# Four-layer transformer block: attention probabilities moved by pairs of units, the last groups' mask and part of their transposes on TensorE, closing steps spread over more units

## Chip, cores and metric

The kernel runs on one core of one Trainium2 chip. The metric is the device time of one execution in microseconds (us); three runs of the kernel before gave a median of 2282.05 us (2280.4 to 2284.7).

## What is computed

The input is x of 1024 tokens by 256 features, float32. Eight sublayers follow each other, each of the form x = layernorm(x + sublayer(x)): four attentions (called attn0 to attn3 here) and four feed-forward layers (ffn0 to ffn3). The change concerns attn1, attn3 and the start of the feed-forward layers. Both attentions have 16 heads of 128 features; attn3 has 4 key/value heads, each shared by 4 query heads, and normalises queries and keys per head.

```python
# attn1 (attn3 alike, with x @ Wq.T, per-head normalisation, k and v repeated, no biases)
logits = jnp.einsum('bhtd,bhds->bhts', q, k) * scale
mask = jnp.triu(jnp.full((t, t), -jnp.inf, dtype=x.dtype), k=1)
weights = jax.nn.softmax(logits + mask, axis=-1)
out = jnp.einsum('bhts,bhsd->bhtd', weights, v)
out = out.transpose(0, 2, 1, 3).reshape(b, t, h * dh)
return out @ Wo + bo
# ffn3: 64 experts, the 8 most probable of each token, and one shared expert
probs = jax.nn.softmax((h @ router_w.T).astype(jnp.float32), axis=-1)
top_vals, top_idx = lax.top_k(probs, TOP_K)
top_vals = top_vals / jnp.sum(top_vals, axis=-1, keepdims=True)
```

The one sequence has 1024 tokens, so a head has 8 blocks of 128 queries, and block b sees b + 1 blocks of keys.

## The kernel before

**Units.** In attn1 and attn3 the work is cut into 128 units each. A unit is one head and one block of 128 queries, with 1 to 8 blocks of keys. attn1 goes through 4 groups g of 4 heads, within a head through the two halves and the 4 blocks of each half. attn3 goes through 4 groups g (one key/value head each), within a group through the 8 blocks b, within a block through the 4 query heads h. Two consecutive units form a pair: in attn1 two neighbouring blocks of a head (n and n + 1 key blocks), in attn3 two heads of one block (equal sizes).

**One unit** (`Pipe.unit`) is a chain over all engines. `scores` (L307) multiplies queries and keys on TensorE into a PSUM tile of two banks, called wide; there are two of them. `exp_scores` adds the causal mask to the last 128 columns on VectorE (L243), takes the row maximum on VectorE (L248), in attn3 multiplies it by a factor on GpSimd (L250), and takes the exponential on ScalarE with the row sum beside it (L253). `norm_probs` takes the reciprocal of the sum on VectorE (L260) and multiplies on GpSimd (L261). `turn_probs` transposes 32x32 squares on VectorE into a tile called turned (L276), and four DMAs on SP's queue (L284) carry it into a tile pt, where it stands fully transposed. In attn1 each unit has its own turned tile and four DMAs (argument `both` false); in attn3 a pair shares one turned tile and four DMAs (`both` true). turned has two buffers. The product with the values (`values`, L298) runs per pair and is copied out by ScalarE (L1131 in attn1, L2050 in attn3).

**Order.** Inside both attentions the order of TensorE, ScalarE, VectorE, GpSimd and SP is the program's own order (`in_order`, transfers included), so an instruction that waits holds up all that follows it on its engine. `unit` emits, for unit u: reciprocal and division of unit u-1, scores of u, mask, maximum and exponential of u, then the transpose of u-1. Then `fill` hands TensorE as much other work as an allowance says (`left`, a base per unit plus a slope per key block): products with values of earlier pairs, output projections (`add_up`, L1107 in attn1; `project_heads`, L758 in attn3), projections of later keys, values and queries. `then` queues a pair's product with the values and frees it five units later (`Pipe.LAG`); a finished group of heads puts its `add_up` on the list `soon`, from which the next unit takes it. When nothing is left to hand out, TensorE has only the scores and the queued products.

**Closing.** In attn3's last group each finished pair of blocks starts a `close`, a generator of which one step runs per unit (`close_on`), one closing after the other: layer norm (L208), transposes of x (`transpose_two`, L173), the router's product (L161), softmax and top 8 on VectorE (L1879 to L1905), and for each of two halves of the experts a split into three bfloat16 parts on VectorE (`split3`, L387 to L389) and, in the same step, their transposes on TensorE (`transpose_comb`, L377). Steps left over when attn3 ends run at the start of ffn3, through the argument `before` of `ffn`.

**Feed-forward.** `ffn` runs chunks of hidden units over the first half of the tokens and, `Kit.LAG` = 2 chunks later, over the second half. Here a scheduler sets the order on each engine; the kernel gives only the program's sequence. ffn1 has a loop of its own with the same LAG.

The helper lines L154, L161 (projections), L173 (transposes) and L307 serve several stages.

Of the kernel before, what the change touches and what calls it, by code (L numbers as in the profile page):

```python
# [24 lines left out]
BF16 = mybir.dt.bfloat16  # L25
# [6 lines left out]
P = 128  # L32
# [4 lines left out]
HALF = 512  # L37
# [5 lines left out]
class Kit:  # L43
# [62 lines left out]
    def constants(self):  # L106
# [8 lines left out]
        make_causal_mask(nc, self.causal, mask_val=NEG)  # L115
        self.ones = const("ones", [P, 1])
# [122 lines left out]
    def exp_scores(self, scores, n, scale=None):  # L239
# [3 lines left out]
        nc.vector.tensor_tensor(  # L243
            scores[:, n - P : n], scores[:, n - P : n], self.causal, ALU.add
        )
# [17 lines left out]
    def turn_probs(self, probs, blocks, pt, slot, both):  # L263

        nc = self.nc
        n = blocks * P  # L270
        if not both or slot == 0:
            self.turned = self.tile("turned", [P, (1 + both) * 2 * HALF])
        squares = self.turned[:, : (1 + both) * n].rearrange(
            "p (b s k q) -> p s b k q", b=4, s=1 + both, q=32
        )
        nc.vector.transpose(  # L276
            squares[:, slot if both else 0],
            probs[:, :n].rearrange("p (k i b) -> p b k i", b=4, i=32),
        )
        if both and slot == 0:  # L280
            return
        slots = slice(0, 2) if both else slice(slot, slot + 1)
        for a in range(4):
            nc.sync.dma_start(  # L284
                out=pt.rearrange("p (s a) r -> p a s r", a=4)[:, a, slots, : n // 4],
                in_=self.turned[a * 32 : a * 32 + 32, : (1 + both) * n].rearrange(
                    "i (b s r) -> i b s r", b=4, s=1 + both
                ),
            )

    def probs_tile(self, blocks):

        n = min(n for n in self.pt_bufs if n >= blocks)
        return self.tile("pt", [P, 8, n * 32], tag=f"pt{n}", bufs=self.pt_bufs[n])

    def values(self, out, value, pt, b, last, first=0):

        self.nc.tensor.matmul(  # L298
            out[:, first * P :].rearrange("p (s q) -> p s q", q=32), lhsT=value,
            rhs=pt[:, first * 4 :, b * 32 : b * 32 + 32], start=b == 0, stop=last,  # L300
        )

    def scores(self, query, key, n):
        s = self.wide()
        for lo in range(0, n, HALF):
            m = min(HALF, n - lo)
            self.nc.tensor.matmul(  # L307
                s[:, lo : lo + m], lhsT=query, rhs=key(lo, m), start=True, stop=True
            )
        return s  # L310
# [3 lines left out]
    LAG = 2  # L314

    def ffn(self, chunks, count, hidden, before=iter(())):
# [8 lines left out]
        def add_up(i, half):  # L325
            size, gate, up, down, more = held[i] if half == 0 else held.pop(i)
            g, u = self.bank()[:size], self.bank()[:size]
            self.project(g, gate, half * HALF, HALF)
            self.project(u, up, half * HALF, HALF)
            h = hidden(g, u, half, more)  # L330
# [6 lines left out]
        for i in range(count + self.LAG):  # L337
# [3 lines left out]
            for _ in before:  # L341
                pass
# [60 lines left out]

COLUMN = 1 / 600


class Pipe:
# [8 lines left out]
    def __init__(self, k, base, slope, more, both=False):  # L416
        self.k, self.base, self.slope, self.more, self.both = k, base, slope, more, both
        self.pairs = 0
        self.soon = []
        self.first, self.rest, self.queued, self.left = None, [], [], 0.0  # L420
# [5 lines left out]
    def unit(self, query, key, blocks, pt, slot, scale=None):  # L426
        k = self.k
        before = self.norm()
        sc = k.scores(query, key, blocks * P)
        probs, inv = k.exp_scores(sc, blocks * P, scale)  # L430
        self.first = (probs, blocks * P, inv, pt, slot)
# [3 lines left out]
    def norm(self):  # L435
        before, self.first = self.first, None
# [5 lines left out]
    def turn(self, before):  # L442
# [5 lines left out]
        for q in self.queued:  # L448
            q[0] -= 1
# [1798 lines left out]
```

## Time and profile before

| what | value |
|---|---|
| median of three runs | 2282.05 us (2280.4 to 2284.7) |
| the profiled execution's own time | 2276.97 us |
| its span, first to last instruction | 2275.3 us |
| TensorE busy (matmul records) | 2065.0 us, 91% |
| VectorE / ScalarE / GpSimd busy | 1325.2 / 856.9 / 528.2 us |
| mean granted TensorE clock | 0.965 of full |
| moved by DMA | 166.74 MB in 200804 packets |

Stages by their own lines: attn0 to about 294 us, ffn0 to about 408, attn1 to about 920, ffn1 to about 985, attn2 to 1214, ffn2 to about 1398, attn3 to about 1895, ffn3 to the end. A float32 matmul appears in the records as two passes, so a 128x512 product is two records. "Idle before" in a row is the time the engine stood before those instructions, and the name after the arrow is what ended it. A busy TensorE isn't a TensorE at full pace: passes are pipelined and a granted clock of 0.5 doubles them.

### The profile page before, as it was taken

How to read it: one execution, taken by the hardware profiler on the slowest of the kernel's cores; microseconds unless marked ns; L12 is line 12 of the kernel's file. 1: busy time of each engine (PE TensorE's matmuls, PEld its weight loads, DVE VectorE, ACT ScalarE, POOL GpSimd, SP SyncE). 2: the span in 40 equal slices, each digit the busy share in tenths (PEclk: the TensorE clock that was granted, in tenths of full speed). 3: DMA queues.
4: the chain of work that ended last, by engine and by line, in shares of the span. 5: the costliest groups of instructions: out<-in, count | busy, mean ns of one | idle time of the engine just before them, and what ended most of it. 6: DMA issues, size and time to landing. Idle time of an engine off the chain costs nothing.

```text
span 2275.3 us, 25208 instructions
## 1 busy us (share of the span) xinstructions
PE 2065.0 (91%) x7955; PEld 1211.8 (53%) x7955; DVE 1325.2 (58%) x2687; ACT 856.9 (38%) x2230; POOL 528.2 (23%) x805
## 2 busy tenths in 40 slices
PE   8999769799999997988888999899998778999997
PEld 4666545466676665754434444466666444444443
DVE  5677646567776777456744444476767774222223
ACT  3666624443343433444452224544443321111111
POOL 4333221333333333402110001333333220000000
PEclk9999879899999999979999999999999989999999
DMA  4100054254545544105000010244445441111100
GB/s 160 36 10 29 29 169 121 65 136 110 139 112 151 151 111 117 38 28 177 2 2 10 28 29 1 48 90 111 96 103 112 104 95 39 37 40 44 30 2 19
DMA packets 200804, 166.74 MB, mean 73 GB/s; under 512 B 71680, under 2 KB 176192, under 8 KB 200672
## 3 DMA queue, kind: packets, MB, share of 16 engines
q1 hardware_dynamic: 191088, 140.07, 24.0%
q0 software_dynamic: 9584, 25.05, 3.7%
q8 instruction: 65, 1.06, 0.2%
q14 instruction: 67, 0.55, 0.1%
HBM read 68.72 MB, written 17.17 MB: 38 GB/s over the span
## 4 chain that ended last, share of the span: by engine, by line
PE 67%; DVE 15%; ACT 6%; DMA 4%; issue 4%; POOL 2%; SPq 1%; DVEq 0%; ACTq 0%; POOLq 0%
PE bank L154 23%; PE wide L307 8%; PE wide L332 8%; PE bank L298 7%; PE bank L161 4%; DVE turned L276 3%; ACT e L692 3%; PE bank L758 2%; DMA pt<-turned 2%; PE bank L1107 2%; PE bank L1544 1%; PE bank L938 1%; PE bank L1282 1%; DVE st L684 1%; PE bank L747 1%
## 5 line engine op out<-in xcount | busy, mean ns | idle before, releaser
L154 PE MATMUL bank<-xT,w 128*128 128x512 f32 (+2 forms) x1520 | 659.8, 567 | 4.1 <-DVE xT L180 2.6
L154 PEld LDWEIGHTS bank<-xT,w 128*128 128x128 f32 (+1 forms) x1520 | 287.9, 194 | 272.6 <-issue 250.7
L276 DVE STREAM_TRANSPOSE turned<-p 128x128 f32<-128x128 f32 (+7 forms) x256 | 312.8, 1222 | 122.1 <-DMA pt<-turned 87.0
L307 PE MATMUL wide<-k,q 128*128 128x512 f32 (+3 forms) x768 | 294.1, 493 | 29.6 <-ACT p L253 28.7
L261 POOL TENSOR_SCALAR p<-p,st 128x128 f32<-128x128 f32 (+7 forms) x256 | 190.4, 744 | 503.0 <-DVE st L260 502.5
L298 PE MATMUL bank<-pt,v 128*128 128x256 f32 x1216 | 282.0, 375 | 7.5 <-DMA pt<-turned 5.0
L298 PEld LDWEIGHTS bank<-pt,v 128*128 128x128 f32 x1216 | 231.5, 194 | 61.9 <-issue 20.0
L307 PEld LDWEIGHTS wide<-k,q 128*128 128x128 f32 x768 | 141.2, 191 | 152.2 <-issue 93.6
L248 DVE TENSOR_REDUCE st<-wide 128x1 f32<-128x128 f32 (+7 forms) x256 | 194.1, 758 | 8.8
L253 ACT ACTIVATE p<-wide,st,factor 128x128 f32<-128x128 f32 (+7 forms) x128 | 106.4, 831 | 235.0 <-POOL st L250 223.7
L2138 DVE TENSOR_TENSOR t<-t,bank 128x512 f32<-128x512 f32 (+1 forms) x66 | 45.4, 688 | 251.6 <-PE bank L154 251.0
L332 PE MATMUL wide<-t,w 128*128 128x512 f32 (+1 forms) x392 | 187.3, 600 | 4.5 <-DVE t L2139 2.8
L253 ACT ACTIVATE p<-wide,st 128x128 f32<-128x128 f32 (+7 forms) x128 | 94.9, 741 | 249.5 <-DVE st L248 229.4
L2137 ACT ACTIVATE t<-bank 128x512 f32<-128x512 f32 (+1 forms) x66 | 39.4, 597 | 306.2 <-PE bank L154 306.2
L161 PE MATMUL bank<-w,xT 128*128 128x512 f32 (+3 forms) x320 | 124.6, 525 | 2.9 <-DVE xT L180 2.9
L243 DVE TENSOR_TENSOR wide<-wide,causal 128x128 f32<-128x128 f32 x256 | 74.2, 290 | 89.7 <-PE wide L307 88.5
L332 PEld LDWEIGHTS wide<-t,w 128*128 128x128 f32 (+1 forms) x392 | 68.2, 189 | 108.6 <-issue 48.1
L692 ACT ACTIVATE e<-wide,st 128x128 f32<-128x128 f32 x256 | 90.1, 377 | 50.9 <-DVE st L684 34.4
L1569 ACT ACTIVATE pt<-wide 128x1024 f32<-128x1024 f32 (+3 forms) x96 | 75.7, 811 | 72.2 <-PE wide L1563 69.9
L161 PEld LDWEIGHTS bank<-w,xT 128*128 128x128 f32 x320 | 59.2, 208 | 48.5 <-issue 42.7
L2131 POOL COPY t<-select 99x128 bf16<-99x128 bf16 (+1 forms) x33 | 9.4, 292 | 319.8 <-PE bank L988 319.8
L235 DVE TENSOR_TENSOR x<-bank,x 128x256 f32<-128x256 f32 x120 | 48.1, 412 | 50.6 <-PE bank L747 21.1
(310 smaller groups left out, 2864.0 us busy)
## 6 DMA issues: line engine op xcount, KB each, us to landing
pt<-turned SPq DMA_DIRECT2D x96, 128.0 KB, 2.8
pt<-turned SPq DMA_DIRECT2D x96, 96.0 KB, 2.4
pt<-turned SPq DMA_DIRECT2D x32, 256.0 KB, 4.9
w<-in_L_ffn_gate_up_dram SPq DMA_DIRECT2D x16, 512.0 KB, 3.7
pt<-turned SPq DMA_DIRECT2D x64, 112.0 KB, 2.5
pt<-turned SPq DMA_DIRECT2D x32, 224.0 KB, 4.4
w<-in_L_attn_Wq_dram SPq DMA_DIRECT2D x12, 512.0 KB, 4.3
w<-in_L_attn_Wo_dram SPq DMA_DIRECT2D x12, 512.0 KB, 3.8
```

The costliest lines, as they stand in the source:

```text
L154: self.nc.tensor.matmul(out, lhsT=weight(c), rhs=self.xcols(c, lo, n), start=c == 0, stop=c == NC - 1)
L161: self.nc.tensor.matmul(out, lhsT=self.xcols(c, lo, n), rhs=weight(c), start=c == 0, stop=c == NC - 1)
L243: nc.vector.tensor_tensor(scores[:, n - P : n], scores[:, n - P : n], self.causal, ALU.add)
L248: nc.vector.tensor_reduce(top, scores[:, :n], axis=AX.X, op=ALU.max, negate=True)
L253: nc.scalar.activation(probs[:, :n], scores[:, :n], AF.Exp, bias=top, scale=1.0 if scale is None else scale, accum_out=total,)
L261: self.nc.gpsimd.tensor_scalar(probs[:, :n], probs[:, :n], total, 1.0, ALU.mult, ALU.mult)
L276: nc.vector.transpose(squares[:, slot if both else 0], probs[:, :n].rearrange("p (k i b) -> p b k i", b=4, i=32),)
L298: self.nc.tensor.matmul(out[:, first * P :].rearrange("p (s q) -> p s q", q=32), lhsT=value, rhs=pt[:, first * 4 :, b * 32 : b * 32 + 32], ...
L307: self.nc.tensor.matmul(s[:, lo : lo + m], lhsT=query, rhs=key(lo, m), start=True, stop=True)
L332: nc.tensor.matmul(acc[m][:, half * HALF : (half + 1) * HALF], lhsT=down[:, m * P : (m + 1) * P], rhs=h, start=i == 0, stop=i == count - 1,)
L692: nc.scalar.activation(e[:, r, f, b, :], sc[:, r, f, b, :], AF.Exp, bias=top[:, at : at + 1], accum_out=total[:, at : at + 1],)
L1569: nc.scalar.activation(two[:, :, lo:], sc[:, :, lo:], AF.Exp)
```

## The change

1. **Pairs.** A class `Pair` replaces `turn_probs`, `probs_tile` and `values`. Both attentions now write the two units of a pair side by side into one turned tile and send four DMAs per pair; in pt the two units lie side by side for each of the four rows of squares, so a DMA's runs are contiguous over the pair. In attn1 that makes 4 DMAs per pair where there were 8. turned is a little larger (15 x 128 and 16 x 128 columns, two buffers), pt a little smaller; attn1 keeps 11 value tiles in place of 12, one tile of the feed-forward weights' decoding is halved, and the order of value projections is shifted by one.
2. **Mask on TensorE.** For g = 3 in both attentions `scores` adds the mask by a bfloat16 product of an identity and the mask into the last 128 columns, and VectorE's addition is left out.
3. **Part of the transposes on TensorE.** For the pairs of head 3 of group 3 in attn1 (4 pairs) and of heads 2 and 3 of group 3 in attn3 (8 pairs) the probabilities are transposed by TensorE, up to four blocks per PSUM bank, and copied into pt by ScalarE; these pairs have neither VectorE transpose nor DMA. The steps run within `fill`, after its first piece of other work.
4. **Closing steps spread.** `close` has one more empty step after the norm, computes both splits in two steps, and only then issues the two transposes, a step each. In `ffn` the left-over steps are taken one after each projection of the first chunks, the rest after the third chunk; before, all were emitted after the first.
5. **Sums over heads two units later.** `soon` holds `[2, add_up]`: a group's output projection is freed two units after its last product, not one.
6. `Kit.LAG` is 3 in place of 2 (ffn1, ffn2, ffn3); a scratch tile of attn3 has one buffer in place of two.

```diff
-    def exp_scores(self, scores, n, scale=None):
+    def exp_scores(self, scores, n, scale=None, masked=False):
-        nc.vector.tensor_tensor(
-            scores[:, n - P : n], scores[:, n - P : n], self.causal, ALU.add
-        )
+        if not masked:
+            nc.vector.tensor_tensor(
+                scores[:, n - P : n], scores[:, n - P : n], self.causal, ALU.add
+            )
...
+        if masked:
+            self.nc.tensor.matmul(
+                s[:, n - P : n], lhsT=self.short_ident, rhs=self.short_causal, start=False,
+                stop=True, skip_group_check=True,
+            )
...
-    LAG = 2
+    LAG = 3
...
             self.project(g, gate, half * HALF, HALF)
+            next(before, None)
             self.project(u, up, half * HALF, HALF)
+            next(before, None)
...
-            for _ in before:
-                pass
+            if i == self.LAG - 1:
+                for _ in before:
+                    pass
...
+class Pair:
...
+    def turn(self, probs, slot):
+        k, n = self.k, self.blocks[slot] * P
+        if slot == 0:
+            self.turned = k.tile("turned", [P, k.turned])[:, : 4 * self.width]
+        squares = self.turned.rearrange("p (b r) -> p b r", b=4)[:, :, self.columns(slot)]
+        k.nc.vector.transpose(
+            squares.rearrange("p b (k q) -> p b k q", q=32),
+            probs[:, :n].rearrange("p (k i b) -> p b k i", b=4, i=32),
+        )
+        if slot == 1:
+            for a in range(4):
+                k.nc.sync.dma_start(
+                    out=self.pt[:, a, : self.width],
+                    in_=self.turned[a * 32 : a * 32 + 32, :].rearrange("i (b r) -> i b r", b=4),
+                )
+    def turn_on_pe(self, probs, slot):
+        k, blocks = self.k, self.blocks[slot]
+        to = self.pt[:, :, self.columns(slot)].rearrange("p a (k q) -> p k a q", q=32)
+        for lo in range(0, blocks, 4):
+            m = min(4, blocks - lo)
+            ps = k.bank()[:, : m * P]
+            for i in range(m):
+                k.nc.tensor.transpose(
+                    ps[:, i * P : (i + 1) * P], probs[:, (lo + i) * P : (lo + i + 1) * P], k.ident
+                )
+            k.nc.scalar.copy(
+                to[:, lo : lo + m], ps.rearrange("p (k a q) -> p k a q", a=4, q=32)
+            )
+            yield m * 0.13
...
     def fill(self):
         while self.left > 0:
             measure = self.step() or self.more()
+            while self.turning:
+                self.left -= self.turn_on()
...
-    k.pt_bufs = {4: 2, 8: 2}
+    k.pt_bufs, k.turned = {7: 2, 15: 2}, 15 * P
...
-            pipe.soon.append(add_up(g, half))
+            pipe.soon.append([2, add_up(g, half)])
...
+                pair = Pair(k, (blocks, blocks + 1), on_pe=(g, h) == (3, 3))
...
             k.norm_tile(t + i, stats[t // 4], rstd[:, i : i + 1])
         yield
+        yield
         k.transpose_two(t)
...
+        parts = [k.tile("t2", [P, 2, 3, 33]) for _ in range(2)]
         for group in range(2):
             yield
-            parts = k.tile("t2", [P, 2, 3, 33])
-            k.split3([parts[:, :, i, :] for i in range(3)], comb[:, :, group, :], [P, 2, 33])
-            k.transpose_comb(parts, k.combT[group], t)
+            k.split3(
+                [parts[group][:, :, i, :] for i in range(3)], comb[:, :, group, :], [P, 2, 33]
+            )
+        for group in range(2):
+            yield
+            k.transpose_comb(parts[group], k.combT[group], t)
...
-            pipe.soon.append(add_up(g, b, oT))
+            pipe.soon.append([2, add_up(g, b, oT)])
...
+                        pair = Pair(k, (b + 1, b + 1), on_pe=(g, h) == (3, 2))
...
-    attn1: dict(q=2, k=5, v=12, pt=2, p4=2, turned=2, ot=7, bv=1, prep=1),
+    attn1: dict(q=2, k=5, v=11, pt=2, p4=2, turned=2, ot=7, bv=1, prep=1),
```

## The prediction

> **What bounds the kernel now.** I read the page first, then the busy time by stage, then TensorE's waits, then the timeline of the worst place. The windows are attn1, attn3 to its last third, the end of attn3, and ffn3; columns are length, busy time and records of PE, PEld, DVE, ACT, POOL, then granted clock, DMA share, GB/s.
>
> ```profile
> 466.00:920.00 454.00, 435.50 (x1664) 301.81 (x1662) 327.59 (x635) 181.60 (x410) 156.62 (x211) 1.00 0.50 126
> ...
> 1440.00:1800.00 360.00, 332.45 (x1246) 217.70 (x1246) 260.27 (x502) 157.35 (x360) 128.51 (x232) 0.99 0.44 95
> 1800.00:1898.00 98.00, 66.97 (x240) 47.62 (x241) 65.42 (x162) 21.36 (x42) 19.43 (x38) 0.86 0.43 106
> 1898.00:2275.00 377.00, 361.03 (x884) 154.72 (x882) 107.88 (x201) 46.84 (x76) 8.43 (x29) 0.99 0.09 28
> ```
>
> TensorE is the bound nearly everywhere. Only the end of attn3 stands out: 31 of 98 us idle, and a clock of 0.86. So added TensorE work costs its full time in most places, and a gain must come from TensorE's idle time. TensorE's own waits name it:
>
> ```profile
> PE wide L307 <- ACT p L253: 28.7, 26, 6.5
> PE bank L377 <- DVE t L389: 28.7, 6, 8.3
> ...
> PE bank L758 <- ACT ot L2050: 8.0, 8, 1.7
> ...
> PE bank L298 <- DMA pt<-turned: 5.0, 4, 1.8
> ```
>
> The second row is the closing: six times TensorE stands in front of a 0.4 us transpose until VectorE has split its data. The first is scores waiting for the softmax chain to free a wide tile. Transfers cost TensorE 5.0 us in the whole kernel, although VectorE waits 87.0 us for them. How a closing stops everything:
>
> ```profile
> 1806.91 0.22 DVE L389 TENSOR_TENSOR t<-t,short 128x66 f32<-128x66 f32 x1
> 1807.19 0.41 PEld L377 LDWEIGHTS bank<-ident,t 128*99 128x99 f32 x2 [7.69 <-DVE t L389]
> 1807.19 0.75 PE L377 MATMUL bank<-ident,t 128*99 128x128 f32 x2 [7.29 <-DVE t L389]
> 1807.52 2.87 PEld L298 LDWEIGHTS bank<-pt,v 128*128 128x128 f32 x8
> 1807.73 3.06 PE L298 MATMUL bank<-pt,v 128*128 128x256 f32 x8
> ```
>
> After 7.29 us of standing, eight value passes take 3.06 us; at 1889.43 the same eight took 1.89. The gap is paid twice.
>
> **The skill.** "TensorE: Matmul & The Clock Gate", Part 1, says the array falls to half clock after an idle window of about 3.4 us and needs about 3.4 us of sustained work to return. The trace agrees: its clock records fall to 0.5 for 6.8 us after the gap of 7.29, for 10.2 us after that of 8.30, in all for 27.3 us in 1780 to 1900. The same page, Part 4, gives about 275 ns for a TensorE transpose in a kernel and says it doesn't count as work for the clock; here the same float32 transposes (L729) have durations of 282 ns but start 109 ns apart in runs of four, and I use 109. "DMA: Bandwidth & Descriptors", Specifications, asks for at least 512 B a transfer; 71680 of the 200804 packets are smaller, and pairs double the runs, but no TensorE time hangs on it. "ScalarE: Activation LUTs" puts a table load at 1283 ns; the trace has 1.28 us.
>
> **Pace.** From the distance of successive starts at full clock: a pass of 512 columns 429 ns, 256 columns 216, 128 columns 109, a bfloat16 product of 128 columns 66 (L1517, the mask product of attn2). A float32 product is two passes. For the two kinds that the change adds the upper bound is busy time by count: L729 20.2 us / 128 = 158 ns, L1517 18.6 / 128 = 145; over 108 transposes and 64 masks that would be 10.3 us more, and I keep it for the range. The lower bound is nothing, where they fall into idle time. "PE work" below is counts times these; "lost" is elapsed less PE work. The profiled execution took 2276.97 us, 5.1 less than the median of 2282.05; I take the saving from both alike.
>
> **A. Last group of attn3** (first row maximum at 1749.8, end of its last projection at 1894.9: 145.1 us). PE work before: scores 4 heads x 36 blocks x 2 x 109 = 30.9 (with rounding); values 31.1 and 9.8 of group 2's last pairs; ten projections of 1.72, 17.2; three closings of 1.8, 5.3: together 94.4. Lost 50.7: five waits of L377 (7.29+3.88+8.30+4.60+1.19 = 25.3), three of L173 on the norm (5.3), one on the copy of xT (2.1), others on ScalarE and one transfer 6.5, and half the 27.3 us at half clock, at most 13.7.
> Added: 32 masks x 66 ns = 2.1; 72 blocks (2 heads x 36) x 109 ns = 7.8. One closing fewer in this stretch (see B), -1.7. PE work after: 102.6.
> Removed from VectorE: 32 masks x 290 ns (row L243) = 9.3; transposes of 16 units, 2 x (0.41+0.63+0.87+1.11+1.33+1.59+1.81+2.03) = 19.6. VectorE is busy 74.4 of the 96.6 us from 1749.8 to 1846.4.
> The chain: VectorE takes a unit's mask only after the reciprocal of the unit before, which waits for its exponential, so a unit lasts mask, maximum, factor, exponential, reciprocal. At six blocks: masks at 1824.61 and 1827.96, 3.35 us, of which 0.6 is a closing's norm. Without mask and norm about 2.5, under TensorE's need in the new order of 2.9 to 3.0 for that size (11.6 for four units). So TensorE becomes the bound, and the closing's splits are made a unit or more ahead of their transposes. What is late next is the division on GpSimd: TensorE's transposes of unit u-1 stand after the scores of u and at most one piece, and wait for exponential, reciprocal (0.15) and division (0.91 at six blocks); behind them wait the next scores. The 16 units' ScalarE copies, some 24 of at most 0.61 us (row L731), stand behind the exponential on ScalarE and hold one or two of four PSUM banks. I allow 14 us lost: a third of the old waits of 14 (L173, xT, others) stays, 5; new waits 16 x 0.35, 5.5; clock 3.5. Bounds 8 (a tenth of the PE work) and 26 (half of the old loss). After: 102.6 + 14 = 116.6. **Saved 28.5** (16.5 to 34.5).
>
> **B. Start of ffn3.** A closing now has 10 to 11 steps, at one per unit, and 8 units per closing come in; so they pile up. The order of the built program confirms it: two closings, not one, stand after the last projection. The first of these lies between the chunks' projections, with some 8 us of them between its router product and its transposes: hidden. The second has its router product followed at once by its transposes on TensorE. Before, that distance was 5.2 us (1901.15 to 1906.36), with 1.94 us of products inside and 3.45 idle. Now about 5.2 idle and 0.7 for a product delayed behind VectorE's route steps, instead of 3.45 and 0.88; half clock follows either way. Loss 1.6, rounded to 2.0, and the closing's own 1.7 moved here. Two more table loads, 2 x 1.28, end under the projections. **Costs 3.7** (0 to 9).
>
> **C. Last group of attn1.** Up to unit 112 (849.5) TensorE never stands (window 800 to 850: no loss), so 16 masks cost 1.1. From 849.5 to 919.3 (69.8 us) PE work is 55.3, lost 14.5, by scores waiting on the chain. Added 16 masks 1.1 and 36 blocks x 109 ns = 3.9: 60.3. VectorE loses 0.29 a unit, and 9.8 of transposes in the last eight units. Lost after 6 (2 to 12): 66.3. Saved 3.5, less 1.1: **2.4** (-3.5 to 6.5).
>
> **D. Sums two units later.** The 8.0 us of L758 on ScalarE's copy: 5.2 lie in groups 0 to 2; three fifths return, **3.0** (0 to 5), since some turn into the wait for the chain.
>
> **E. Pairs.** In attn1 groups 0 to 2 TensorE loses 1.3 and 2.4 us of 108 (556 to 664, 664 to 772). VectorE's shorter waits gain nothing there. Transfers are later: a pair's values come four units after its transpose, some 14 us at 3.6 a unit, while transpose (2.0) and landing (4.9 for 256 KB, row of DMA issues) need 7. SP has 240 issues in attn1 for 512; its other issues move up. **0** (-3 to 3).
>
> **F. LAG 3**: the same chunks in the same steady order; ffn3 from 1920 to 2230 already loses only 0.2 us. **0** (-2 to 2).
>
> Sum: 28.5 - 3.7 + 2.4 + 3.0 = 30.2. Profiled 2246.8; median **2251.9**.
>
> **Rivals.** (1) New waits take half: transposes on TensorE wait 0.8 us in each of 24 units, 19 in place of 5.5 and 3: saving 20, time 2262 to 2270. For it: chain and TensorE are within a fifth of each other. Against: the PE-bound units let the division finish. (2) Slower: each of these 24 transposes is reached before its unit's exponential has started to be read, and TensorE stands through exponential, reciprocal and division, about 2.4 us at six blocks: 24 x 2.4 = 58, in place of 8.5, time about 2301. It decides against the change from 1.6 us per unit (30.2 / 24 on top of 0.35). Against: scores of u, mask and a piece of 1.7 us lie between. (3) The pile at ffn3's start exposes both closings, about 12 us more with clock: 2264. (4) VectorE's 87 us for transfers did hold attn1 back: its other 8.7 us lost (466 to 800) and most of the 6 in C go too: 2239. That the mask isn't moved is excluded by the instruction order.
>
> **Chances.** Forecast, 2238 to 2264: 0.68. Rival 1: 0.15. Rival 2: 0.04. Rival 3: 0.06. Rival 4: 0.07. Range 2238 to 2269: 2 in 10 left out. A measurement can tell 0.2% (4.6 us) from no change. Faster: 0.67 + 0.13 + 0.05 + 0.07 = 0.92; same 0.04; slower 0.04 (rival 2).
>
> **What would show it.** A right: waits of the comb transposes on the splits under 8 us in all, clock over 0.95 in attn3's last group, its stretch near 117 us, new waits of transposes on GpSimd near 0.35 us. B: one gap of about 5 us at ffn3's start. C: scores' waits on the exponential in attn1's end under 6. D: projections waiting on ScalarE's copy under 3 us. Wrong if the wait on the exponential grows past 28.7, or the division holds TensorE for over 1.6 us a unit.

## The result and the profile after

The changed kernel takes 2273.26 us (median of seven runs, 2268.97 to 2276.67). The kernel before, on the same chip beside it, takes 2280.40 us (seven runs, 2277.2 to 2285.86). The ratio is 0.9966, with a 95% interval of 0.9952 to 0.998: faster by some 7 us, where 30 were forecast. The profiled executions say the same, 2268.97 us against 2276.97, so they can be taken apart. Cut at the first row maximum of each group and at the last output projection of an attention:

| stretch | before, us | after, us | difference | forecast |
|---|---|---|---|---|
| start to attn1 | 440.7 | 442.7 | +2.0 | 0 |
| attn1, groups 0 to 2 | 348.2 | 351.5 | +3.3 | 0 (E) |
| attn1, last group | 130.5 | 139.5 | +9.0 | -2.4 (C) |
| ffn1, attn2, ffn2 | 509.4 | 509.6 | +0.2 | 0 (F) |
| attn3, groups 0 to 2 | 321.1 | 321.9 | +0.8 | -3.0 (D) |
| attn3, last group | 145.3 | 116.8 | -28.5 | -28.5 (A) |
| ffn3 | 380.2 | 385.2 | +5.0 | +3.7 (B) |

The last group of attn3 came out as forecast. Attn1 gave 12.3 us of it away, where a small gain was forecast. The first row is no effect of the change: over the kernels below, whose code is the same there, it lay between 439.5 and 444.0 us. The fourth varies as much, 505.8 to 515.0 us over the kernels with `Kit.LAG` 3 in every layer, at granted clocks of 0.98 to 0.95, and the lag's own 3 us (below) are lost in it. Attn1's four groups together took 490.8 to 494.0 us in four kernels that leave attn1 as changed, and 476.5 to 479.6 in five that have it as before (the kernel before among them), so a difference of one or two us between two executions is no finding.

The busy times by stage of the changed kernel, in the columns of the prediction's first fence: the last group of attn1, the last group of attn3, ffn3.

```profile
794.20:933.70 139.50, 127.05 (x528) 90.91 (x527) 77.00 (x147) 46.66 (x108) 46.23 (x66) 0.95 0.35 85
1765.10:1881.90 116.80, 105.78 (x492) 79.15 (x492) 70.84 (x180) 46.76 (x112) 33.80 (x74) 0.99 0.32 83
1881.90:2267.10 385.20, 367.59 (x906) 158.90 (x904) 115.41 (x238) 50.88 (x81) 9.28 (x32) 0.98 0.09 28
```

Attn3's end now runs at 0.99 of the clock and stands 11 of 117 us. It is attn1's last group that has the low clock, 0.95, and stands 12.5 us.

TensorE's waits in the changed kernel, longest in total first (engine and line, what it waited for: us in all, times, longest):

```profile
PE wide L274 <- ACT p L259: 17.5, 18, 6.5
PE bank L421 <- POOL p L267: 14.8, 7, 6.1
...
PE bank L439 <- DMA pt<-turned: 12.0, 11, 2.1
...
PE bank L353 <- DVE t L365: 5.2, 1, 5.2
PE wide L307 <- DVE t L1878: 4.8, 2, 2.4
...
PE bank L2041 <- ACT t L2033: 3.8, 4, 1.2
```

Row by row against before: scores that wait for the exponential fell from 28.7 to 17.5 us; the closing's transposes (L377 then, L353 now) from 28.7 in six waits to one of 5.2; output projections that waited for ScalarE's copy (L758, 8.0) are gone from the list. Four rows are new or grown: TensorE's own transposes wait 14.8 us for GpSimd's division, values wait 12.0 us for transfers instead of 5.0, ffn2's products 4.8 instead of 1.6 (L307, L332 before), and attn3's sums of squares 3.8 for ScalarE (L2041). Much of what the closings and the scores gave back, other waits took.

### The profile page after: what moved, and what is told of

It reads as the page before. It is cut to its first block, busy times and chain, and to the rows that moved or that the text cites. A ratio compares the mean times of both kernels' runs of the same rounds, so it can differ in the third digit from the quotient of the medians.

```text
span 2267.1 us, 24836 instructions
## 1 busy us (share of the span) xinstructions
PE 2073.2 (91%) x8127; PEld 1221.8 (54%) x8127; DVE 1284.3 (57%) x2599; ACT 872.9 (39%) x2268; POOL 528.9 (23%) x807
## 2 busy tenths in 40 slices
DMA packets 124255, 159.60 MB, mean 70 GB/s; under 512 B 28928, under 2 KB 96064, under 8 KB 124128
## 3 DMA queue, kind: packets, MB, share of 16 engines
q8 instruction: 65, 1.06, 0.2%
## 4 chain that ended last, share of the span: by engine, by line
PE 70%; DVE 13%; ACT 6%; DMA 4%; issue 3%; POOL 2%; SPq 2%; DVEq 0%; ACTq 0%; POOLq 0%
PE bank L159 23%; PE wide L274 8%; PE bank L439 8%; PE wide L307 8%; PE bank L166 4%; ACT e L749 3%; DMA pt<-turned 3%; DVE turned L402 2%; PE bank L1164 2%; PE bank L815 2%; PE bank L1601 1%; DVE st L741 1%; PE bank L995 1%; PE bank L1339 1%; POOL p L267 1%
## 5 line engine op out<-in xcount | busy, mean ns | idle before, releaser
L402 DVE STREAM_TRANSPOSE turned<-p 128x128 f32<-128x128 f32 (+7 forms) x232 | 283.6, 1223 | 84.2 <-DMA pt<-turned 48.2
L274 PE MATMUL wide<-k,q 128*128 128x512 f32 (+3 forms) x768 | 294.3, 493 | 18.4 <-ACT p L259 17.5
L307 PE MATMUL wide<-t,w 128*128 128x512 f32 x392 | 187.6, 601 | 8.2 <-DVE t L1878 4.8
L2201 DVE TENSOR_TENSOR t<-t,bank 128x512 f32<-128x512 f32 x66 | 45.3, 687 | 247.2 <-PE bank L159 247.2
L2200 ACT ACTIVATE t<-bank 128x512 f32<-128x512 f32 x66 | 39.4, 597 | 294.1 <-PE bank L159 279.7
L307 PEld LDWEIGHTS wide<-t,w 128*128 128x128 f32 x392 | 68.2, 189 | 113.4 <-issue 48.3
L249 DVE TENSOR_TENSOR wide<-wide,causal 128x128 f32<-128x128 f32 x192 | 55.9, 291 | 97.7 <-PE wide L274 96.4
```

Of the source, the lines that this page charges most:

```text
L249: nc.vector.tensor_tensor(scores[:, n - P : n], scores[:, n - P : n], self.causal, ALU.add)
L274: self.nc.tensor.matmul(s[:, lo : lo + m], lhsT=query, rhs=key(lo, m), start=True, stop=not masked or lo + m < n, skip_group_check=masked,)
L307: nc.tensor.matmul(acc[m][:, half * HALF : (half + 1) * HALF], lhsT=down[:, m * P : (m + 1) * P], rhs=h, start=i == 0, stop=i == count - 1,)
L402: k.nc.vector.transpose(squares.rearrange("p b (k q) -> p b k q", q=32), probs[:, :n].rearrange("p (k i b) -> p b k i", b=4, i=32),)
```

## The experiments

After the result two accounts were open. The theory: attn3's gain is the spread closing alone, and attn1 loses by two things, transposes on TensorE that wait for the division (C) and transfers by pairs that arrive later (E). The rivals: attn3 owes its gain to mask and transposes on TensorE; and attn1 loses by the added TensorE work, or by the eleven value tiles and the shifted order, rather than by waits. All twelve kernels are edits of the changed kernel; each ratio is to the kernel before, run on the same chip, so whole kernels are compared by their ratios. The code cuts show the lines that name an edit; what else it needs (the argument `alone` and its branch, shown once, buffer sizes, the lines of an edit described above) is left out at the dots. "Attn1" below is its four groups together, 478.6 us before and 490.9 after; all stretches are of profiled executions.

### Attn1's transposes back on VectorE

```diff
-                pair = Pair(k, (blocks, blocks + 1), on_pe=(g, h) == (3, 3))
+                pair = Pair(k, (blocks, blocks + 1))
```

> The changed kernel, but in attn1's last head the transposes are VectorE's and DMAs' again; attn3's stay on TensorE. Theory G (GpSimd's queue): in attn1 the changed kernel loses 6.05 and 2.78 us of TensorE where transposes wait for a division that stands behind the weights' decoding on GpSimd, some 5 us of half clock after them, and 3.9 us of passes. Without them attn1's last group falls from 139.5 us to about 128, and the kernel is 8 to 12 us faster than the changed one (2262 to 2266). Rival T (late transfers of pairs cost attn1 its time): nothing changes or it gets slower, since four more pairs go by DMA: 2272 to 2277.

Measured 2264.01 us, ratio to the kernel before 0.9948 (0.9928 to 0.9968). Attn1 took 489.8 us, its last group 136.2 instead of 139.5. The kernel's waits, for the two rows that matter:

```profile
PE bank L439 <- DMA pt<-turned: 13.1, 11, 1.9
...
PE bank L421 <- POOL p L267: 5.5, 4, 2.9
```

The waits for the division fell from 14.8 to 5.5 us (what is left lies in attn3), yet the last group gained only 3.3 us, where the theory had some 11. Its waits for transfers rose from 1.6 to 3.6 us, and the last values waited 3.3 more, which the trace puts down to VectorE (L213), although the last pair's fourth transfer had landed only 0.2 us before they started. So the transposes on TensorE are not the whole loss; without them the pairs take their place.

### Attn1's transfers unit by unit, transposes on TensorE kept

```diff
...
+        if self.alone:
+            turned = k.tile("turned", [P, k.turned])[:, : 4 * n // 4]
+            k.nc.vector.transpose(
...
+            for a in range(4):
+                k.nc.sync.dma_start(
+                    out=self.pt[:, a, self.columns(slot)],
+                    in_=turned[a * 32 : a * 32 + 32, :].rearrange("i (b r) -> i b r", b=4),
+                )
+            return
...
-                pair = Pair(k, (blocks, blocks + 1), on_pe=(g, h) == (3, 3))
+                pair = Pair(k, (blocks, blocks + 1), on_pe=(g, h) == (3, 3), alone=True)
```

> The changed kernel, but attn1 sends each unit's transposed squares by itself again, four DMAs per unit from a turned tile of its own. Rival T: TensorE's waits of value products for transfers fall from 12.0 us towards the 5.0 of before and groups 1 and 2 of attn1 get back to 113.8 and 119.5 us: 4 to 7 us faster, 2266 to 2269. Theory G: transfers matter little, 0 to 3 us either way, 2270 to 2275, and the gap of 6.05 us in the last head stays.

Measured 2267.67 us, 0.9969 (0.9954 to 0.9985). Attn1 489.2 us: its groups 1 and 2 were 1.9 and 1.4 us shorter than in the changed kernel, the last group one us longer (140.5). Waits for transfers fell from 12.0 to 5.5 us, those for the division stayed at 14.5. So without transfers by pairs, the transposes on TensorE keep the last group as long as it was, while groups 0 to 2 are back near the kernel before (348.7 against 348.2). Either cause alone keeps attn1 nearly as long as both: they overlap in the last group.

### The weights' decoding moved on GpSimd

Attn1's steps of decoding are taken one and two in turn, so that GpSimd's multiplication and DMA issue come earlier than the last units.

```diff
-            for _ in range(2 if count % 4 == 3 else 1):
+            for _ in range(1 + count % 2):
```

> The changed kernel, but the decoding of the feed-forward weights beside attn1 goes on at 1.5 steps a unit, not 1.25, so that it ends near unit 105 and GpSimd has only divisions in the last head. Theory G: the wait of 6.05 us for the division falls under 3 us, attn1's last group is 4 to 7 us shorter, kernel 2266 to 2270. If the wait is simply the chain of exponential, reciprocal and division, it stays at 6 and the time at 2271 to 2275.

Measured 2268.35 us, 0.9969 (0.9956 to 0.9981). The longest wait of a transpose for the division fell from 6.1 to 3.5 us, and attn1's last group from 139.5 to 134.9 us, but its first rose from 112.3 to 120.3; attn1 in all 491.6. So the decoding on GpSimd did stand ahead of the division at the worst place; moved earlier it costs as much elsewhere. But 3.5 us of the wait stay with nothing of the decoding ahead, and this kernel's timeline shows by what:

```profile
884.65 0.12 DVE L266 RECIPROCAL st<-st 128x1 f32<-128x1 f32 x1
...
885.29 0.33 PE L421 MATMUL bank<-ident,p 128*128 128x128 f32 x1 [3.53 <-POOL p L267]
```

GpSimd stood for 2.16 us before this division, waiting for the reciprocal. The unit's exponential was done at 882.1, but on VectorE the transpose of the unit before it, of eight blocks, stood ahead of the reciprocal until 884.7.

### The closing as before, all else changed

```diff
...
-            if i == self.LAG - 1:
-                for _ in before:
-                    pass
+            for _ in before:
+                pass
...
-        yield
-        parts = [k.tile("t2", [P, 2, 3, 33]) for _ in range(2)]
...
+            parts = k.tile("t2", [P, 2, 3, 33])
+            k.split3([parts[:, :, i, :] for i in range(3)], comb[:, :, group, :], [P, 2, 33])
+            k.transpose_comb(parts, k.combT[group], t)
```

> The changed kernel with the closing as it was: split and transposes in one step, no empty step after the norm, and in the feed-forward layer all left-over steps after the first chunk. If the spread closing is what shortened attn3's last group from 145.1 to 116.8 us, it grows by 15 to 25 us and the kernel takes 2285 to 2298. If mask and transposes on TensorE did it, the group stays under 125 us and the kernel under 2280.

Measured 2296.31 us, 1.0093 (1.0071 to 1.0114): slower than the kernel before. Attn3's last group took 140.0 us instead of 116.8, and the old wait is back, in this kernel's list and in its timeline (start, length, engine, line, and in brackets the idle time before and what ended it):

```profile
PE bank L350 <- DVE t L362: 23.1, 7, 4.4
```

```profile
1868.08 0.22 DVE L362 TENSOR_TENSOR t<-t,short 128x66 f32<-128x66 f32 x1
...
1868.44 0.72 PE L350 MATMUL bank<-ident,t 128*99 128x128 f32 x2 [4.36 <-DVE t L362]
```

Split and transpose stand 0.14 us apart, with TensorE idle for 4.36 us before. The spread closing is worth 23 us in this group of the changed kernel. With the old closing, transposes and mask on TensorE and the later sums together make attn3's last group 5.3 us shorter than before; what the transposes add to the spread one, attn3's transposes on VectorE (below) shows.

### LAG 2

```diff
-    LAG = 3
+    LAG = 2
```

> The changed kernel with a lag of 2 chunks between the halves of the tokens in the feed-forward layers, as before. In the changed kernel two waits at the end of ffn2 are 2.39 us each where they were 0.78, which the lag can explain. If so, 2 to 4 us are saved between attn1 and attn3, and ffn3 keeps its 385 us or loses up to 3 us, as the second half then needs its closing earlier: 0 to 4 us faster than the changed kernel. If the lag has no part, both stretches stay within 1 us.

Measured 2267.76 us, 0.9971 (0.996 to 0.9981). The two waits of ffn2 (L307 on L1878) fell from 2.4 us each to 0.8, and ffn3 grew from 385.2 to 388.8 us. By the waits LAG 3 costs some 3 us in ffn2. What it saves in ffn3 is less sure: the left-over closing steps are emitted after chunk `LAG`, so this edit moves them too, and the other kernel with LAG 2 there (the spread closing alone, below) took 386.5 us, where those with LAG 3 took 383.3 to 385.8.

### Attn3's transposes back on VectorE

```diff
-                        pair = Pair(k, (b + 1, b + 1), on_pe=(g, h) == (3, 2))
+                        pair = Pair(k, (b + 1, b + 1))
```

> The changed kernel, but the transposes of attn3's last group are all VectorE's and DMAs' again; mask on TensorE and spread closing stay. If the spread closing is nearly all of the gain in that group, the group stays at 115 to 121 us: no change. If the 19.6 us less on VectorE were needed, it grows to 126 to 132 us, kernel 10 to 15 us slower than the changed one.

Measured 2269.35 us, 0.9978 (0.9968 to 0.9988). Attn3's last group: 117.2 us, against 116.8 with transposes on TensorE. The 19.6 us that VectorE is spared and the 7.8 that TensorE is given, by the prediction's count, cancel to 0.4. In that stretch 6.2 us of waits for the exponential and 3.0 for a closing stand in place of 8.2 behind GpSimd.

### Attn1 as before

Transfers by units, mask and transposes on VectorE, twelve value tiles in the old order, sums over heads at the next unit; everything else, the layout of pt too, is the changed kernel.

```diff
...
-            pipe.soon.append([2, add_up(g, half)])
+            pipe.soon.append([1, add_up(g, half)])
...
-                pair = Pair(k, (blocks, blocks + 1), on_pe=(g, h) == (3, 3))
+                pair = Pair(k, (blocks, blocks + 1), alone=True)
...
-                masked=g == 3,
...
-    attn1: dict(q=2, k=5, v=11, pt=2, p4=2, turned=2, ot=7, bv=1, prep=1),
+    attn1: dict(q=2, k=5, v=12, pt=2, p4=2, turned=2, ot=7, bv=1, prep=1),
```

> attn1 as in the kernel before (transfers and turned tiles per unit, mask and all transposes on VectorE, sums one unit later, 12 value tiles, the old order of value projections); attn3 and the feed-forward layers as changed. If attn1's own changes cost the 12 us by which its stretch grew (478.7 to 491.0 us from first maximum to last projection), it is back at 478 to 481 and the kernel 9 to 13 us faster than the changed one, some 18 us faster than before. If the 12 us are an accident of one execution (the clock), it stays within 4 us of the changed one.

Measured 2257.18 us, 0.9917 (0.9901 to 0.9934). Attn1 477.5 us, as before the change (478.6). So attn1's own parts of the change cost it 13 us, and the rest of the change costs attn1 nothing.

### Pairs alone in attn1

The same, but with the pairs kept, and with them the eleven value tiles and the shifted order.

```diff
-            pipe.soon.append([2, add_up(g, half)])
+            pipe.soon.append([1, add_up(g, half)])
...
-                pair = Pair(k, (blocks, blocks + 1), on_pe=(g, h) == (3, 3))
+                pair = Pair(k, (blocks, blocks + 1))
...
-                masked=g == 3,
```

> The changed kernel, but attn1 keeps of its changes only the transfers by pairs (with 11 value tiles and the shifted order): mask and all transposes on VectorE, sums one unit later. Theory T: transfers by pairs alone cost attn1 5 to 8 us, stretch 484 to 487, waits of value products for transfers near 12 us in the kernel. Theory G with the rest: pairs cost 0 to 2 us, stretch 478 to 481.

Measured 2264.57 us, 0.9959 (0.9944 to 0.9973). Attn1 487.0 us, 9.5 more than the kernel above, in all four groups but the first. In attn1 TensorE waited 10.4 us for transfers, where the kernel above waited 3.3; and in the last group the clock was 0.95 where it was 0.99 above. The largest wait is in the drain after the last unit, by this kernel's timeline:

```profile
905.94 2.03 DVE L402 STREAM_TRANSPOSE turned<-p 128x1024 f32<-128x1024 f32 x1 [1.25 <-POOL p L267]
908.03 3.88 SPq L408 DMA_DIRECT2D pt<-turned  x4
...
915.20 5.03 PE L439 MATMUL bank<-pt,v 128*128 128x256 f32 x11 [3.95 <-DMA pt<-turned]
```

The last transpose is done at 907.97. SyncE then takes 3.88 us to issue the four transfers, and the values start at 915.20, 7.2 us after the transpose. In the next kernel, with transfers by units, the same step started 4.8 us after a transpose done at 901.77:

```profile
906.54 3.48 PE L451 MATMUL bank<-pt,v 128*128 128x256 f32 x16 [1.76 <-DMA pt<-turned]
```

### Eleven value tiles and the shifted order, transfers by units

As the kernel with attn1 as before, but with eleven value tiles and the shifted order. Against pairs alone it differs in the transfers by units only, and in the turned tile that is sized for one unit.

```diff
...
-    k.pt_bufs, k.turned = {7: 2, 15: 2}, 15 * P
+    k.pt_bufs, k.turned = {7: 2, 15: 2}, 8 * P
...
-                pair = Pair(k, (blocks, blocks + 1), on_pe=(g, h) == (3, 3))
+                pair = Pair(k, (blocks, blocks + 1), alone=True)
```

> attn1 as in the kernel before but for 11 value tiles and the shifted order of value projections; the rest as changed. It parts the two things that e8 (pairs with 11 tiles and shifted order) kept together. Theory T (the pair's transfer itself lands late): attn1's stretch 476 to 480 us as in e7, ratio to before 0.990 to 0.993. Rival R (the room taken for the larger tiles costs): stretch 483 to 487, ratio 0.995 to 0.997.

Measured 2252.74 us, 0.9905 (0.9888 to 0.9923). Attn1 475.9 us. The value tiles and the order cost nothing, so the 9.5 us (11.1 against this kernel) belong to the pairs.

### The spread closing alone

Attn1 as before, and in attn3 neither mask nor transposes on TensorE, sums at the next unit, LAG 2. Of the change there stay the spread closing, attn3's pairs (pairs before too, in another layout) and the smaller scratch tiles.

```diff
-    LAG = 3
+    LAG = 2
...
-            pipe.soon.append([2, add_up(g, b, oT)])
+            pipe.soon.append([1, add_up(g, b, oT)])
...
-                        pair = Pair(k, (b + 1, b + 1), on_pe=(g, h) == (3, 2))
+                        pair = Pair(k, (b + 1, b + 1))
```

> The kernel before with the spread closing as the one change that can matter: attn1 as before, attn3 with mask and transposes on VectorE, sums one unit later and a lag of 2 chunks; the pair's layout in attn3 stays. If the spread alone makes the gain of attn3's last group, that group takes 115 to 122 us (145 before, 117 changed) and the kernel is 20 to 26 us faster than before, ratio 0.989 to 0.991. If the mask on TensorE is needed too, the group takes 125 us or more, ratio 0.993 or more.

Measured 2253.54 us, 0.9902 (0.9886 to 0.9918). Attn3's last group took 117.0 us: the whole gain of step A, with no mask and no transpose on TensorE. Its waits of TensorE show the rows of scores and projections as before, and a short one of the closing:

```profile
PE wide L274 <- ACT p L259: 31.1, 27, 6.5
...
PE bank L827 <- ACT ot L2124: 11.6, 11, 2.0
...
PE bank L353 <- DVE t L365: 10.7, 2, 6.7
```

The 31.1 us of scores waiting for the exponential are no less than the 28.7 of before, and yet the kernel is 22 us faster. It was the closing's row that cost the time: 28.7 us in six waits before, here one of 4.0 in attn3 and one of 6.7 at ffn3's start; the clock of attn3's last group is 0.96, where it was 0.91 before.

### What the runs point to

Attn1 as before, LAG 2 in ffn2 only; attn3 as in the changed kernel.

```diff
...
+    k.LAG = 2
...
+    k.LAG = 3
...
```

> e7 (attn1 as before, attn3 as changed) with a lag of 2 chunks in ffn2 alone. e5 showed ffn2's two late waits at 0.78 in place of 2.39 us with lag 2, and ffn3 3.6 us longer. So ffn2 should give 3 us and ffn3 stay at 385: ratio to before 0.989 to 0.991, the best so far. If ffn2's 3 us come back later, it equals e7 (0.9917).

Measured 2247.95 us, 0.9882 (0.9863 to 0.9901), the lowest ratio of all, though its interval overlaps those of the two kernels above, so the three are not told apart. Attn1 479.6 us, attn3's last group 115.6.

### The same with attn3's sums at the next unit

```diff
...
-            pipe.soon.append([2, add_up(g, b, oT)])
+            pipe.soon.append([1, add_up(g, b, oT)])
...
```

> e11 with attn3's sums over heads one unit later again in place of two. In the changed kernel the 8.0 us of waits for the copy before the sums are gone, yet groups 0 to 2 of attn3 took 321.9 us for 321.2. If the later sums only moved the wait, groups 0 to 2 stay within 1.5 us and the closing, which starts a unit earlier, takes up to 3 us from ffn3's start: same as e11 or up to 3 us faster. If the later sums do help, groups 0 to 2 grow by 3 to 6 us.

Measured 2255.50 us, 0.9914 (0.9899 to 0.9929). Groups 0 to 2 of attn3 took 321.0 us against 322.6, so the later sums are worth nothing there. The last group took 121.1 against 115.6. Its projections waited only 1.4 us for ScalarE's copies; what grew is the transposes' wait for the division, all of it in this group:

```profile
PE bank L433 <- POOL p L267: 12.0, 8, 2.8
```

In the kernel above that row has 5.5 us, and 2.7 more behind GpSimd's other step (L1975). With the transposes on TensorE the later sums are worth some 5 us in the last group; with them on VectorE the group took 117.0 with sums at the next unit. Why the earlier sums lengthen the waits for the division was not tried.

## Why the prediction was wrong, by its own steps

**A, right in its sum, wrong in its reason.** ("Lost" is, as in the prediction, elapsed time less TensorE's work at full pace.) Forecast 116.6 us, 14 lost; measured 116.8, 15 lost at the same paces (101.8 of TensorE work against 102.6 forecast). But the prediction let VectorE's relief carry part of the gain, and the runs show the closing alone does it: 117.0 without mask and transposes on TensorE, 117.2 with the mask, but no transposes, on TensorE. The mechanism is to be seen in the changed kernel's timeline, at a closing:

```profile
1829.91 0.22 DVE L365 TENSOR_TENSOR t<-t,short 128x66 f32<-128x66 f32 x1
...
1831.44 0.41 PE L353 MATMUL bank<-ident,t 128*99 128x128 f32 x2
```

The split ends 1.31 us before TensorE takes it, and the product has no idle time in brackets. Before, the same product stood 7.29 us. The new waits for the division are 5.5 us, as allowed for (16 x 0.35), but in four places of up to 2.9 us; that the sum agrees is luck. A fifth of 2.7 is put down to another step of GpSimd (L1962). In place of them, with transposes on VectorE, stood 6.2 us for the exponential and 3.0 for one closing, so the two arrangements come out equal.

**B, right.** One gap at ffn3's start, 5.23 us, where about 5.2 were forecast:

```profile
1907.53 0.22 DVE L365 TENSOR_TENSOR t<-t,short 128x66 f32<-128x66 f32 x1
...
1907.56 1.18 PE L353 MATMUL bank<-ident,t 128*99 128x128 f32 x4 [5.23 <-DVE t L365]
```

It cost 5.0 us instead of 3.7: the moved closing brought 16 passes of 128 columns or fewer, 1.7 us at 109 ns each, as in the sum, so 3.3 us were lost where the sum had 2.0.

**C, wrong: a loss of 9 us in attn1's last group for a gain.** The step took "Lost after 6 (2 to 12)" of TensorE where 14.5 had been lost. The added work was 6 us, near the 6.1 of the sum; but lost were 19.6 over the whole last group, where before lost 16.6. So 6 of the 9 us are the added passes themselves, which the spared VectorE was to pay for, and 3 are time lost on top. The changed kernel's timeline at the worst place:

```profile
880.50 1.12 POOL L267 TENSOR_SCALAR p<-p,st 128x1024 f32<-128x1024 f32 x1 [2.28 <-DVE st L266]
...
881.58 1.28 POOL L1839 TENSOR_TENSOR decoded<-sign,scales 128x512 f32<-128x512 f32 x1
881.65 2.00 DVE L402 STREAM_TRANSPOSE turned<-p 128x1024 f32<-128x1024 f32 x1 [1.06 <-POOL p L267]
883.58 0.12 DVE L266 RECIPROCAL st<-st 128x1 f32<-128x1 f32 x1
...
885.32 0.61 POOL L1844 DMA_DIRECT2D decoded_down<-decoded  x1 [2.46 <-issue]
885.97 0.82 POOL L267 TENSOR_SCALAR p<-p,st 128x128 f32<-128x128 f32 x2
...
886.40 0.47 PE L421 MATMUL bank<-ident,p 128*128 128x128 f32 x1 [6.05 <-POOL p L267]
```

TensorE's last product before it ended at 880.35. One transpose of 0.47 us holds all of TensorE for 6.05 us. The division it needs takes 0.4 us, and two queues delay it in turn. The unit has one block and its exponential was done at 881.1, but on VectorE its reciprocal stands behind the transpose of the unit before, of eight blocks, until 883.7: 3.4 of the 6.05 us. Then on GpSimd the weights' decoding and its DMA issue stand ahead (1.28 us, 2.46 of standing, 0.61), and the division starts at 885.97, 2.3 us later than the reciprocal allowed. With the transposes on VectorE, it is VectorE that waits for this division. The prediction looked at this chain only at six blocks of attn3 and only for reciprocal and division; it didn't follow VectorE's and GpSimd's own queues in attn1, where a large unit is followed by a small one and the decoding runs. A second wait, 2.78 us, is the drain's, where no other work is left to put in between. Both went with half clock, and the gain expected from a spared VectorE couldn't show: scores' waits on the exponential did fall, in attn1's last group from 10.1 us to 1.5, as forecast (under 6), and 9.4 us on the division took their place.

The earlier decoding (6.1 to 3.5 us, and 4.6 us off the last group) shows that GpSimd's queue is the cause of 2.5 us of the longest wait; the 3.5 that stay are, by both timelines, the reciprocal behind VectorE's transpose, which no run tried to move. What GpSimd waits for in the 2.46 us before its issue stays open.

**E, wrong: a loss of 8 to 11 us taken alone, forecast at nothing.** The step said "a pair's values come four units after its transpose, some 14 us at 3.6 a unit, while transpose (2.0) and landing (4.9 for 256 KB, row of DMA issues) need 7". Both numbers, the 7 and the 14, were off. The changed kernel's timeline where a large pair is followed by small units:

```profile
643.79 2.04 DVE L402 STREAM_TRANSPOSE turned<-p 128x1024 f32<-128x1024 f32 x1 [0.72 <-POOL p L267]
...
645.90 7.61 SPq L408 DMA_DIRECT2D pt<-turned  x8
...
654.61 0.88 DVE L402 STREAM_TRANSPOSE turned<-p 128x384 f32<-128x384 f32 x1 [3.99 <-DMA pt<-turned]
654.62 1.75 PE L439 MATMUL bank<-pt,v 128*128 128x256 f32 x7 [1.61 <-DMA pt<-turned]
```

and the transfers of that window in the changed kernel (duration of an issue in ns and time to landing), and the landing in the kernel before, from 630 to 660 us:

```profile
L408 SPq DMA_DIRECT2D pt<-turned x8: 543/755/1482, 645.9 to 652.9; - x8
...
DMA to landing us min/median/max: 3.1/4.2/4.9
```

```profile
DMA to landing us min/median/max: 1.8/2.5/3.5
```

From the transpose's start to the product 10.8 us pass (8.8 from its end), not 7. A landing of 4.2 us is that of one transfer; all four wait for the pair's second transpose, and SyncE issues them in turn, in 0.54, 0.61, 1.06 and 1.48 us, so that the fourth is out 3.8 us after the first was begun. By units, about half of the data had left a unit earlier, in pieces that land in 2.5. And the units that follow have one to four blocks and come at 1.5 to 2.0 us each where nothing holds them (the row maxima of 256, 384 and 512 columns start at 646.45, 647.95 and 649.93), so TensorE stands ready for the values at 653.0, 9.2 us after the transpose's start, not 14. "3.6 a unit" is the mean of a group whose units grow from one block to eight. VectorE stands 3.99 us at the same time, for a turned tile that stays taken until the pair's transfers have landed.

How C and E share the 12.3 us: groups 0 to 2 have no transposes on TensorE, so their 3.3 are E's (back to 0.5 with transfers by units). In the last group the 9.0 are C's (10.0 with transfers by units). Taking C away gave only 3.3 there, since pairs turned by TensorE aren't transferred, and once they are, the drain waits for the pairs: 5.4 us more than before with pairs alone. So pairs alone cost attn1 8.4 us against before, TensorE's share (mask and transposes, with the later sums) alone 10.6, both 12.3. The mask has little part in it: pairs with the mask on VectorE and pairs with it on TensorE left the last group at 135.9 and 136.2 us.

**D, wrong by 3 us.** Projections waiting for ScalarE's copy went, as forecast, from 8.0 us to none listed. Groups 0 to 2 of attn3 got no shorter (321.1 to 321.9), and with the sums put back at the next unit they were 321.0. "Three fifths return" had no ground: of these groups' waits 5.2 us went, but 3.6 for ScalarE in another row (L2041) came, and those for transfers rose from 1.0 to 2.9. The gain it has is in the last group, 5.5 us, inside A.

**F, right in its sum, not in its parts.** LAG 3 costs 3.2 us of waits in ffn2, and the changed kernel's ffn3 was 1.3 and 3.6 us shorter than that of the two kernels with LAG 2 there.

**The rivals.** Rival 1's kind of wait came, but in attn1 rather than attn3 and by other means; its range, 2262 to 2270, missed the time by 3 us for another reason. Rival 2's mechanism, a standing TensorE before a transpose, occurred in 7 places with 14.8 us, not 24 with 58. Rival 3's pile cost 5.0 us, not 12. Rival 4, that VectorE's waits for transfers hold attn1 back, is not borne out: VectorE's waits for transfers fell from 87.0 to 48.2 us in the whole kernel, and attn1 grew longer in each of the runs with pairs.

The steps that failed are C and E, both in attn1, and, by less, D. In sum: A 0, B 1.3, C and E 14.7 (12.3 lost where 2.4 were to be gained), D 3.8, start and middle 2.2 short of the forecast: 22.0 us, which is the 30.2 forecast less the 8.2 of span measured.

## What to carry to other kernels

A consumer that stands because its producer is issued just ahead of it is mended by distance in the order, and that was all the gain here; moving work to the bound engine beside it added nothing measurable in attn3, and in attn1 its own passes and new waits. When a step is moved to another engine, follow everything that is queued ahead of its input on the other engines, not only the step's own chain. When transfers are merged, count from the last producer through the issue of all pieces to the landing of the last, and set it against the shortest units that follow, not against the mean.

## What the runs showed of the hardware

- Four transfers of 240 KB each were issued by SyncE one after another in 0.54 to 1.48 us, and landed in 4.3 us (median) after their issue. Fewer and larger packets didn't help: 200804 became 124255, those under 512 B fell from 71680 to 28928, and TensorE's waits for transfers grew from 5.0 to 12.0 us.

- A wait of 2.78 us (before the eight transposes of attn1's drain, at 910.19) went with half clock, though the idle window that the prediction took from the Trainium skill ("TensorE: Matmul & The Clock Gate", Part 1) is about 3.4 us. All changes of this trace's clock record lie multiples of 3.413 us apart, so TensorE's busy time (the number after the length) can be read against the clock (the third from the end) for each such window of the changed kernel:

```profile
397.58:400.99 3.41, 1.50 (x7) 0.76 (x5) 3.20 (x7) 2.97 (x5) 0.00 (x0) 1.00 0.35 122
...
906.16:909.57 3.41, 0.98 (x7) 0.74 (x7) 1.16 (x2) 2.07 (x5) 0.77 (x2) 1.00 0.01 2
909.57:912.98 3.41, 2.79 (x11) 2.61 (x12) 0.00 (x0) 1.19 (x3) 0.57 (x1) 0.50 0.02 5
1407.93:1411.34 3.41, 2.46 (x17) 1.55 (x15) 2.20 (x7) 1.87 (x2) 0.00 (x0) 1.00 0.00 0
1411.34:1414.74 3.40, 0.73 (x6) 0.31 (x4) 3.36 (x13) 0.30 (x1) 0.00 (x0) 1.00 0.00 0
```

After 1.50 us of busy time, all of it products, the clock was 0.50 in the next window; after 0.98 us, all of it seven transposes, it was 0.50; after 2.46 us, of which 2.02 were transposes, it stayed at 1.00. So in these windows a fall went with how much of the window TensorE was busy, and no full window of idleness was needed. Part 4 of the same page says that transposes don't count as work for the clock in the same way; the third of these windows, with 0.44 us of products, kept the full clock all the same, where the first, with 1.50, lost it.

- A DMA issue on GpSimd took 0.61 us after 2.46 us of standing, and what was queued behind it, a division of 0.4 us, started 2.3 us after its reciprocal was done, with TensorE waiting.
